# Strassen's product for an attention block's output projection, a third PSUM bank pair for the scores, and a bias added later

## The chip, the cores and the metric

The kernel runs on one core of one Trainium2 chip. Time is the device's microseconds from the first to the last instruction of one execution; the comparisons use several executions of each kernel. A core has TensorE (PE; matrix products, whose weight loads are listed apart as PEld), VectorE (DVE), ScalarE (ACT), GpSimd (POOL), and SyncE (SP), which here issues all transfers between memory and the on-chip buffer SBUF. TensorE writes to PSUM, which has eight banks of 128 x 512 float32; the kernel uses them as four pairs.

## The reference, cut to what matters

Two layers follow one another, on a batch of 8 images of 512 channels and 32 x 32 = 1024 tokens, all in float32:

```python
def layer(x, gn_w, gn_b, qkv_w, qkv_b, proj_w, proj_b):      # x: 8 x 512 x 1024
    xn = groupnorm(x) * gn_w + gn_b                          # 8 groups in layer 0, 32 in layer 1
    q, k, v = split(qkv_w @ xn + qkv_b)                      # each 512 x 1024, 8 heads of 64
    p = softmax(q_h^T k_h / 8)                               # per head, 1024 x 1024
    o_h = v_h p^T                                            # 64 x 1024 per head
    return proj_w @ o + proj_b + x                           # 512 x 512 times 512 x 1024
```

One image in one layer is a *unit*; there are 16. The matmuls of one unit are three projections of 512 x 512 by 512 x 1024, the attention of eight heads, and the output projection of the same size.

## The kernel before

Each unit runs in three stages: q, k and v; then the output projection of the unit before it; then this unit's attention. The output projection is late by one stage so that its last inputs, which need a transfer, have time to arrive.

q, k and v are computed by one level of Strassen's product (Winograd's form): the weights and the input are cut into 2 x 2 blocks and combined, seven block products are made instead of eight, and the outputs are sums of them. `blocks` does this for all three; `left` and `right` hold the seven operands on each side.

```python
    def blocks(name, left, right, tokens, c11, others, done):
        bx, by, bz = apair[0], sbank[0], sbank[1]
        def products(bank, k, start, stop):
            a, b = left[k], right[k]
            for i in range(4 if tokens else 2):
                # ... dst: a half of the bank pair
                for c in range(2):
                    at, moving = (b, a) if tokens else (a, b)
                    nc.tensor.matmul(dst, at[:, c, ts(i, P)], moving[:, c, :], ...)     # L284
            done()
        products(bx, 1, True, False)
        p1 = work(accpool, "acc", "p1")
        nc.scalar.copy(p1, bx)
        products(by, 6, True, False)
        u2 = work(trpool, "tr", "u2")
        nc.vector.tensor_add(u2, by, p1)
        products(bx, 2, False, True)
        c11(bx)
        products(by, 7, False, False)
        u3 = work(ppool, "p", "u3")
        nc.vector.tensor_add(u3, by, p1)
        products(bz, 5, True, False)
        others(1, 1, bz, u3)
        products(by, 4, False, True)
        others(1, 0, by, p1)
        products(bz, 3, False, True)
        others(0, 1, bz, u2)
```

The output projection is a plain product: four row blocks by two halves of the tokens, each the sum of four matmuls, and each evacuated with bias and residual in one VectorE instruction.

```python
    def project(w, after):
        for o in range(CC):                       # CC = 4
            for h in range(NH):                   # NH = 2
                bank = turns[2 + g % 2 + 4 * (g // 2 % 2)]
                for c in range(CC):
                    nc.tensor.matmul(bank, w.wproj[:, c, ts(o, P)], w.ao[c][:, ts(h, FD)],   # L381
                                     start=(c == 0), stop=(c == CC - 1))
                cols = w.res[o][:, ts(h, FD)]
                w.evac = nc.vector.scalar_tensor_tensor(                                      # L389
                    cols, bank, vec[:, l, PB, o : o + 1], cols, ALU.add, ALU.add)
                after(g)                          # the next unit's group statistics, one at a time
                g += 1
            nc.sync.dma_start(dst[o * P : (o + 1) * P, :], w.res[o])                          # L394
```

The residual's four tiles come from `ppool`, four buffers of 128 x 1024, which also hold the exponentials of attention and the `u3` of q, k and v. The last unit has no stage after it; `project_last` (L403) makes all sums but the last of four terms first, while the last inputs are prepared.

Attention has 64 steps: eight chunks (a pair of heads, half of the queries) of eight key blocks (`t`). A step makes scores for its keys, their exponential on ScalarE, and, one step later, the product with v. Scores alternate between two bank pairs; products of a chunk accumulate in one of the other two.

```python
        def scores(s):
            bank = sbank[s % 2]
            before = [state["exp"][s - 2]] if s >= 2 else []
            if s == 0:
                before += w.last["q"] + w.last["k"]
            gate(*before)
            # four matmuls of 64 x 64 x 512                                                   # L440
            p = ppool.tile([P, 2, FD], F32, tag="p", name=f"p_{u}_{s}")
            state["exp"][s] = nc.scalar.activation(p, bank, AF.Exp, scale=SCALE)              # L448
            return p
        # products(s, p): four matmuls of 64 x 64 x 512 into apair[c % 2]                     # L467
        # summed(s, p): sums of the exponentials on VectorE                                   # L484, L486
        # evacuate(c): ScalarE copy (L492) and VectorE addition (L493) into w.ao
        prev = None
        for s in range(n_chunks * NT):
            c, t = divmod(s, NT)
            p = scores(s)
            if prev is not None:
                products(s - 1, prev)
            if t == 0 and c > 0:
                evacuate(c - 1)
                transposed(c - 1)                                                             # L499
            if t == 2 and c > 0:
                reduced(c - 1)                    # L509; after a pair of chunks: transfers L515
            if c % NH == 1 and t == 0 and c > 1:
                reciprocals(c // NH - 1)          # small VectorE work, transfers L537, L542
            if c % NH == 1 and t == 6 and c > 1:
                divide(c // NH - 1)                                                           # L549
            if c % NH == 1 and t == 7 and 1 < c < n_chunks - 1:
                add_bias(c // NH - 1, 0)          # ScalarE, V's bias                         # L556
            if c % NH == 0 and t == 1 and c > 2:
                add_bias(c // NH - 2, 1)
            summed(s, p)
            at_step(s, state)                     # the next unit's group norm, a piece a step
            prev = p
        products(n_chunks * NT - 1, prev)
        evacuate(n_chunks - 1)
```

`at_step` makes the next unit's means (chunk 0, step 3) and variances (chunk 0, step 6) by small matmuls (L193), its scales in chunk 1, and applies them in chunks 2 to 5.

The end of the program, after the last unit's attention:

```python
    old.res = load_res(old.u)                     # four transfers, L109
    old.wproj = wproj
    project_last(old, rest)
```

Of the kernel before, what the change touches and what calls it, by code (L numbers as in the profile page):

```python
# [18 lines left out]
P = 128  # L19
# [13 lines left out]
def fast_path(ctx, tc, x, qkv_wT, proj_wT, vecs, groups, out, flag):  # L33
# [12 lines left out]

    nc = tc.nc
# [8 lines left out]
    BL = 32  # L56
# [9 lines left out]
    aopool = pool("aopool", CC)  # L66
# [7 lines left out]
    rbpool = pool("rbpool", 2)  # L74
# [56 lines left out]
    def mix_weights(l, mats, engine):  # L131
# [4 lines left out]
        for i, a in enumerate(mats):  # L136
# [13 lines left out]
    def mix_x(u, xn):  # L150

        b11, b12 = xn[:, :2, :FD], xn[:, :2, FD:]
        b21, b22 = xn[:, 2:, :FD], xn[:, 2:, FD:]
        t1, t2, t4 = (
            tpool.tile([P, 2, FD], F32, tag=f"t{k}", name=f"t{k}_{u}") for k in (1, 2, 4)
        )
        sub = nc.vector.tensor_sub
        parts = (
            lambda: sub(t1, b12, b11), lambda: sub(t2, b22, t1),
            lambda: sub(t4, b21, t2), lambda: sub(b12, b22, b12),  # L160
        )
        return {1: b11, 2: b21, 3: b22, 4: t4, 5: t1, 6: t2, 7: b12}, parts

    def load_proj(l):
        w = wpool.tile([P, CC, C], F32, tag="wproj", name=f"wproj_{l}")
        nc.sync.dma_start(w, proj_wT[l].rearrange("(c p) o -> p c o", p=P))
        return w
# [100 lines left out]
    def blocks(name, left, right, tokens, c11, others, done):  # L268
# [3 lines left out]
        bx, by, bz = apair[0], sbank[0], sbank[1]  # L272

        def products(bank, k, start, stop):
# [14 lines left out]
            done()  # L289

        def work(pool, tag, k):
            return pool.tile([P, 2, FD], F32, tag=tag, name=f"{k}_{name}")
# [3 lines left out]
        nc.scalar.copy(p1, bx)  # L296
        products(by, 6, True, False)
        u2 = work(trpool, "tr", "u2")
        nc.vector.tensor_add(u2, by, p1)
        products(bx, 2, False, True)  # L300
        c11(bx)
        products(by, 7, False, False)
        u3 = work(ppool, "p", "u3")
        nc.vector.tensor_add(u3, by, p1)
        products(bz, 5, True, False)
        others(1, 1, bz, u3)
        products(by, 4, False, True)
        others(1, 0, by, p1)
        products(bz, 3, False, True)
        others(0, 1, bz, u2)  # L310

    def projections(w, rest):
# [7 lines left out]
        def done():  # L320
            nonlocal g
            g += 1
            for part in rest.get(g, ()):
                part()

        for sel, bias in (("q", QB), ("k", KB)):
# [24 lines left out]
            blocks(f"{sel}_{u}", left, w.right, False, c11, others, done)  # L351
# [17 lines left out]
        blocks(f"v_{u}", w.lefts[2], w.right, True, v11, v_others, done)  # L369

    def project(w, after):
# [5 lines left out]
        for o in range(CC):  # L377
            for h in range(NH):
                bank = turns[2 + g % 2 + 4 * (g // 2 % 2)]
                for c in range(CC):  # L380
                    nc.tensor.matmul(  # L381
                        bank,
                        w.wproj[:, c, ts(o, P)],
                        w.ao[c][:, ts(h, FD)],
                        start=(c == 0),
                        stop=(c == CC - 1),
                    )
                cols = w.res[o][:, ts(h, FD)]
                w.evac = nc.vector.scalar_tensor_tensor(  # L389
                    cols, bank, vec[:, l, PB, o : o + 1], cols, ALU.add, ALU.add  # L390
                )
                after(g)
                g += 1
            nc.sync.dma_start(dst[o * P : (o + 1) * P, :], w.res[o])  # L394

    def project_last(w, rest):
# [4 lines left out]
        def products(g, c):  # L401
            o, h = divmod(g, NH)
            nc.tensor.matmul(  # L403
                turns[g], w.wproj[:, c, ts(o, P)], w.ao[c][:, ts(h, FD)],
# [17 lines left out]
    def attention(w, at_step):  # L422
# [3 lines left out]
        w.ao = [aopool.tile([P, N], F32, tag="ao", name=f"ao_{u}_{pr}") for pr in range(CC)]  # L426
        n_chunks = CC * NH
        state = {"exp": {}, "free": [[], []], "acc": {}}

        def scores(s):  # L430
            c, t = divmod(s, NT)
            pr, qh = divmod(c, NH)
            bank = sbank[s % 2]
            before = [state["exp"][s - 2]] if s >= 2 else []
            if s == 0:
                before += w.last["q"] + w.last["k"]
# [11 lines left out]
            state["exp"][s] = nc.scalar.activation(p, bank, AF.Exp, scale=SCALE)  # L448
            return p

        def products(s, p):
# [4 lines left out]
            if s == 0 and w.evac_before is not None:  # L456
                before.append(w.evac_before)
            if t == 0:
                before += state["free"][c % 2]
            if s == 0:  # L460
                before += w.last["v"]
# [26 lines left out]
        def evacuate(c):  # L488
# [4 lines left out]
            i1 = nc.vector.tensor_add(w.ao[pr][:, ts(qh, FD)], banks[1], tmp)  # L493
# [26 lines left out]
        def reciprocals(pr):  # L520
            def work(name):
                return small.tile([BL, 2 * BL], F32, tag=name, name=f"{name}_{u}_{pr}")
# [24 lines left out]
        def divide(pr):  # L547
            col = u * CC + pr
            nc.vector.scalar_tensor_tensor(  # L549
                w.ao[pr], w.ao[pr], 1.0, state["rb"], ALU.mult, ALU.mult,  # L550
# [3 lines left out]
        def add_bias(pr, h):  # L554
            cols = w.ao[pr][:, ts(h, FD)]
# [4 lines left out]
        prev = None  # L560
        for s in range(n_chunks * NT):
            c, t = divmod(s, NT)
            p = scores(s)
            if prev is not None:
                products(s - 1, prev)
# [9 lines left out]
            if c % NH == 1 and t == 7 and 1 < c < n_chunks - 1:  # L575
                add_bias(c // NH - 1, 0)
            if c % NH == 0 and t == 1 and c > 2:
                add_bias(c // NH - 2, 1)
            summed(s, p)
            at_step(s, state)  # L580
            prev = p
        products(n_chunks * NT - 1, prev)
# [12 lines left out]
        return lambda: reciprocals(CC - 1), divide_last  # L595
# [5 lines left out]
    mats = load_weights(0)  # L601
    wproj = load_proj(0)
# [356 lines left out]
```

## Time and profile before

| | |
|---|---|
| time of three executions | 3423.61, 3425.54, 3425.72 us (median 3425.54) |
| span of the profiled execution | 3422.5 us, TensorE's granted clock 0.999 |
| matmuls L467, products with v | 8192 records, 1118.3 us busy |
| matmuls L440, scores | 8192 records, 1116.1 us busy |
| matmuls L381, output projection | 960 records, 414.4 us busy |
| exponentials L448 | 1024, mean 1024 ns |
| additions L486 | 768, mean 1223 ns |
| biased evacuations L389 (128 x 512) | 120, mean 750 ns |
| additions L493 (128 x 512) | 128, mean 688 ns |
| V's bias L556 | 128, mean 720 ns |
| store of 256 KB, issue to landing | 2.0 us median |
| store of 512 KB, issue to landing | 2.6 us median |

A float32 matmul appears as two records. The spacing of starts, not the length of a record, is what a matmul costs in a stream, because matmuls overlap. Idle time in a row of the profile names what ended it; time that the chain of waits gives to TensorE can only be shortened by giving TensorE less to do.

### The profile page before, as it was taken

How to read it: one execution, taken by the hardware profiler on the slowest of the kernel's cores; microseconds unless marked ns; L12 is line 12 of the kernel's file. 1: busy time of each engine (PE TensorE's matmuls, PEld its weight loads, DVE VectorE, ACT ScalarE, POOL GpSimd, SP SyncE). 2: the span in 40 equal slices, each digit the busy share in tenths (PEclk: the TensorE clock that was granted, in tenths of full speed). 3: DMA queues.
4: the chain of work that ended last, by engine and by line, in shares of the span. 5: the costliest groups of instructions: out<-in, count | busy, mean ns of one | idle time of the engine just before them, and what ended most of it. 6: DMA issues, size and time to landing. Idle time of an engine off the chain costs nothing.

```text
span 3422.5 us, 50906 instructions
## 1 busy us (share of the span) xinstructions
PE 3381.2 (99%) x21122; PEld 1679.7 (49%) x21122; DVE 2211.3 (65%) x2790; ACT 1374.0 (40%) x1533; POOL 32.6 (1%) x32
## 2 busy tenths in 40 slices
PE   8999999999999999999999999999999999999999
PEld 4445454454544545455454554545445454454543
DVE  4865938658385583856838568384673946749466
ACT  1632606336062360723517235172451714417144
POOL 0000000000000000001000000000000000000000
PEclk9999999999999999999999999999999999999999
DMA  2111020111101111012120111101111011110102
GB/s 76 36 35 56 21 74 20 32 56 27 68 20 32 56 33 68 15 32 93 39 74 15 32 63 33 62 15 38 56 33 62 15 38 56 33 62 15 38 32 70
DMA packets 57674, 148.21 MB, mean 43 GB/s; under 512 B 19808, under 2 KB 20064, under 8 KB 57440
## 3 DMA queue, kind: packets, MB, share of 16 engines
q1 hardware_dynamic: 57440, 144.90, 12.6%
q8 instruction: 171, 2.80, 0.3%
q14 instruction: 63, 0.52, 0.0%
HBM read 109.21 MB, written 34.08 MB: 42 GB/s over the span
## 4 chain that ended last, share of the span: by engine, by line
PE 96%; DVE 1%; ACT 1%; issue 1%; DMA 1%; SPq 0%; POOL 0%; DVEq 0%
PE a L467 25%; PE s L440 25%; PE s L284 24%; PE a L381 12%; PE a L284 10%; ACT p L448 1%; DVE acc L486 0%; DMA xn<-x_dram 0%; DMA drec<-rec 0%; DVE tr L499 0%; DVE stats L181 0%; DMA rb<-drec 0%; PE s L403 0%; PE a L403 0%; PE a L193 0%
## 5 line engine op out<-in xcount | busy, mean ns | idle before, releaser
L448 ACT ACTIVATE p<-s 128x1024 f32<-128x1024 f32 x1024 | 1046.9, 1024 | 1159.2 <-PE s L440 1149.5
L467 PE MATMUL a<-p,v 64*64 64x512 f32 x8192 | 1118.3, 590 | 15.8 <-ACT p L448 13.7
L440 PE MATMUL s<-q,k 64*64 64x512 f32 x8192 | 1116.1, 590 | 0.3 <-DVE v L364 0.3
L486 DVE TENSOR_TENSOR acc<-acc,p 128x1024 f32<-128x1024 f32 x768 | 938.9, 1223 | 118.0 <-ACT p L448 77.4
L467 PEld LDWEIGHTS a<-p,v 64*64 64x64 f32 x8192 | 385.3, 131 | 524.2 <-ACT p L448 406.8
L440 PEld LDWEIGHTS s<-q,k 64*64 64x64 f32 x8192 | 413.6, 133 | 450.2 <-issue 449.1
L381 PE MATMUL a<-ao,wproj 128*128 128x512 f32 x960 | 414.4, 592 | 0.0
L381 PEld LDWEIGHTS a<-ao,wproj 128*128 128x128 f32 x960 | 182.4, 190 | 223.2 <-issue 222.4
L389 DVE SCALAR_TENSOR_TENSOR x<-a,vec,x 128x512 f32<-128x512 f32 x120 | 90.1, 750 | 272.8 <-PE a L381 272.8
L284 PE MATMUL a<-xn,w 128*128 128x512 f32 x512 | 234.0, 600 | 4.0 <-DVE xn L241 4.0
L284 PEld LDWEIGHTS a<-xn,w 128*128 128x128 f32 x512 | 96.8, 191 | 132.4 <-issue 113.0
L484 DVE TENSOR_TENSOR acc<-p,p 128x1024 f32<-128x1024 f32 x128 | 153.2, 1197 | 11.3 <-ACT p L448 11.3
L499 DVE STREAM_TRANSPOSE tr<-acc 128x1024 f32<-128x1024 f32 x128 | 158.0, 1235 | 0.0
L509 DVE TENSOR_REDUCE red<-tr 128x32 f32<-128x1024 f32 x128 | 154.4, 1207 | 0.6
L556 ACT ACTIVATE ao<-ao,vec 128x512 f32<-128x512 f32 x128 | 89.1, 720 | 110.3 <-DVE ao L549 110.3
L493 DVE TENSOR_TENSOR ao<-a,tmp 128x512 f32<-128x512 f32 x128 | 88.1, 688 | 60.1 <-ACT tmp L492 60.1
L296 ACT COPY p_k<-a 128x1024 f32<-128x1024 f32 x16 | 16.2, 1012 | 254.4 <-PE a L284 254.4
L296 ACT COPY p_v<-a 128x1024 f32<-128x1024 f32 x16 | 16.2, 1012 | 251.8 <-PE a L284 235.8
L284 PE MATMUL a<-w,xn 128*128 128x256 f32 x512 | 115.7, 379 | 0.0
L284 PE MATMUL s<-xn,w 128*128 128x512 f32 x256 | 115.1, 592 | 0.0
L284 PE MATMUL s<-t,s2w 128*128 128x512 f32 x256 | 115.1, 592 | 0.0
L284 PE MATMUL s<-t,w 128*128 128x512 f32 x256 | 115.1, 592 | 0.0
(100 smaller groups left out, 2167.6 us busy)
## 6 DMA issues: line engine op xcount, KB each, us to landing
rb<-drec SPq DMA_DIRECT2D x128, 256.0 KB, 3.9
xn<-x_dram SPq DMA_DIRECT2D x32, 512.0 KB, 4.8
x<-x_dram SPq DMA_DIRECT2D x32, 512.0 KB, 3.2
mid<-x SPq DMA_DIRECT2D x32, 512.0 KB, 2.6
xn<-mid SPq DMA_DIRECT2D x32, 512.0 KB, 4.9
x<-mid SPq DMA_DIRECT2D x32, 512.0 KB, 3.5
out_dram<-x SPq DMA_DIRECT2D x28, 512.0 KB, 2.6
w<-qkv_wT_dram SPq DMA_DIRECT2D x6, 1024.0 KB, 11.4
```

Of the source, the lines that this page charges most:

```text
L284: nc.tensor.matmul(dst, at[:, c, ts(i, P)], moving[:, c, :], start=start and c == 0 and not (tokens and i % 2), stop=stop and c == 1, skip ...
L381: nc.tensor.matmul(bank, w.wproj[:, c, ts(o, P)], w.ao[c][:, ts(h, FD)], start=(c == 0), stop=(c == CC - 1),)
L389: w.evac = nc.vector.scalar_tensor_tensor(cols, bank, vec[:, l, PB, o : o + 1], cols, ALU.add, ALU.add)
L440: nc.tensor.matmul(bank[e * H : (e + 1) * H, j, :], w.k[pr][j * H : (j + 1) * H, t * P + e * H : t * P + (e + 1) * H], w.q[pr][j * H : (j ...
L448: state["exp"][s] = nc.scalar.activation(p, bank, AF.Exp, scale=SCALE)
L467: nc.tensor.matmul(banks[r][j * H : (j + 1) * H, :], w.v[rows, t, lo : lo + D], p[rows, j, :], start=(t == 0), stop=(t == NT - 1),)
L484: nc.vector.tensor_add(acc, state["first"], p)
L486: nc.vector.tensor_add(acc, acc, p)
L493: i1 = nc.vector.tensor_add(w.ao[pr][:, ts(qh, FD)], banks[1], tmp)
L499: nc.vector.transpose(tr, state["acc"].pop(c))
L509: nc.vector.tensor_reduce(red[:, :, qh, :], state["tr"].rearrange("p j (f i) -> p j f i", i=BL), AX.X, ALU.add)
L556: nc.scalar.activation(cols, cols, AF.Identity, bias=vec[:, units[u][0], VB, pr : pr + 1])
```

## The change

The output projection (all units but the last) goes through `blocks` as well: seven block products in place of eight. The right operand's combinations (`mix_right`) are made on VectorE while k is computed, the weights' ones once per layer, and the bias and the residual are added to the partial sums in SBUF. Results are stored in halves. The combinations overwrite one block of the weights, so the last unit, which keeps the plain product, loads its weights again.

```diff
-        bx, by, bz = apair[0], sbank[0], sbank[1]
+        bx, by, bz = apair[0], sbank[0], apair[1]
...
     def project(w, after):
...
-        for o in range(CC):
-            for h in range(NH):
... (the plain product and its evacuation, shown above)
+        def plus(to, o, cols, more):
+            return nc.vector.scalar_tensor_tensor(
+                to, cols, vec[:, l, PB, o : o + 1], more, ALU.add, ALU.add
+            )
+        def done(sums):
+            nonlocal g
+            g += 1
+            for i in range(2):
+                if g == 2:
+                    u2 = sums[1][:, i, :]
+                    plus(u2, i, w.res[i][:, FD:], u2)
+                elif g == 4:
+                    u3 = sums[2][:, i, :]
+                    plus(u3, 2 + i, w.res[2 + i][:, FD:], u3)
+                elif g == 5:
+                    p1 = sums[0][:, i, :]
+                    plus(p1, 2 + i, w.res[2 + i][:, :FD], p1)
+            after(g)
+        def store(o, h):
+            nc.sync.dma_start(dst[o * P : (o + 1) * P, ts(h, FD)], w.res[o][:, ts(h, FD)])
+        def c11(bank):
+            for i in range(2):
+                cols = w.res[i][:, :FD]
+                plus(cols, i, bank[:, i, :], cols)
+                store(i, 0)
+        def others(r, h, bank, more):
+            for i in range(2):
+                o = 2 * r + i
+                w.evac[h] = nc.vector.tensor_add(
+                    w.res[o][:, ts(h, FD)], bank[:, i, :], more[:, i, :]
+                )
+                store(o, h)
+        w.evac = [None, None]
+        blocks(f"o_{w.u}", w.left, w.right_o, False, c11, others, done, (rbpool, "rb"))
```

Attention's first six scores rotate through three bank pairs, and the products follow two steps behind in the first chunk; the last score goes to a free pair ahead of two products. This lets exponentials run ahead where the pipeline fills and empties. V's bias moves from the steps around a chunk's start to steps 2 and 3, and the group statistics' small matmuls move from chunk 0 to chunk 1, because their bank pair is the one borrowed.

```diff
-            bank = sbank[s % 2]
-            before = [state["exp"][s - 2]] if s >= 2 else []
+            if s < 6:
+                bank = (*sbank, apair[1])[s % 3]
+                before = state["exp"][s - 3 : s - 2] if s >= 3 else []
+            elif s == n_steps - 1:
+                bank = apair[0]
+                before = state["free"][0]
+            else:
+                bank = sbank[s % 2]
+                before = [state["exp"][s - (3 if s < 8 else 2)]]
             if s == 0:
-                before += w.last["q"] + w.last["k"]
+                before = before + w.last["q"] + w.last["k"] + (w.evac_before[:1] or w.last["v"])
+            elif s == 2:
+                before = before + w.evac_before
...
+        follow = {s: [s - 1] for s in range(NT, n_steps)}
+        follow.update({s: [s - 2] for s in range(2, NT - 1)})
+        follow[NT - 1] = [NT - 3, NT - 2]
+        follow[n_steps - 2] = []
+        follow[n_steps - 1] = [n_steps - 3, n_steps - 2]
...
-            if c % NH == 1 and t == 7 and 1 < c < n_chunks - 1:
-                add_bias(c // NH - 1, 0)
-            if c % NH == 0 and t == 1 and c > 2:
-                add_bias(c // NH - 2, 1)
+            if c % NH == 0 and t in (2, 3) and c > 2:
+                add_bias(c // NH - 2, t - 2)
...
-        return lambda: reciprocals(CC - 1), divide_last
+        w.right_o, mixing = mix_right(f"o_{u}", *w.ao)
+        return {4: [lambda: reciprocals(CC - 1)], 10: [divide_last], 12: mixing[:2], 14: mixing[2:]}
...
-            project(old, lambda g: stats_of(g - 2))
+            stats_after = {3: (0, 1, 2), 4: (3,), 6: (4, 5), 7: (6, 7)}
+            project(old, lambda g: stats_of(*stats_after.get(g, ())))
...
-            if c == 0 and t == 1:
+            if c == 1 and t == 1:
                 aggregate()
-            elif c == 0 and t == 3:
-                means(abank[2 * pair], *(free or [w.evac_before]))
+            elif c == 1 and t == 3:
+                means(abank[2 * pair], *free)
-            elif c == 0 and t == 6:
+            elif c == 1 and t == 5:
                 variances(abank[2 * pair], *free)
...
     old.res = load_res(old.u)
-    old.wproj = wproj
-    project_last(old, rest)
+    old.wproj = load_proj(1, "w0")
+    project_last(old, [part for g in (4, 10) for part in rest[g]])
```

The keys 4, 10, 12 and 14 count block products of q, k and v (seven each): the last pair's reciprocals, its division, and the two halves of the mixing are placed there. The attention outputs `w.ao` become two tiles of 128 x 2 x 1024, and the working tile `u3` of the projection takes the buffer of the broadcast reciprocals (`rbpool`), which goes from two buffers to one.

## The prediction

> **What bounds the kernel now.** I read the page's busy times and its chain of waits first, then busy time by stage, then the order of time at the seams between stages.
>
> ```profile
> PE 3381.2 (99%) x21122; PEld 1679.7 (49%) x21122; DVE 2211.3 (65%) x2790; ACT 1374.0 (40%) x1533; POOL 32.6 (1%) x32
> ...
> PE a L467 25%; PE s L440 25%; PE s L284 24%; PE a L381 12%; PE a L284 10%; ACT p L448 1%; DVE acc L486 0%; DMA xn<-x_dram 0%; DMA drec<-rec 0%; DVE tr L499 0%; DVE stats L181 0%; DMA rb<-drec 0%; PE s L403 0%; PE a L403 0%; PE a L193 0%
> ```
>
> TensorE is the bound: 99% busy, and 96% of the chain. The chain's shares name what can be shortened: attention (L440, L467) half, the q, k and v products (L284) a third, the output projection (L381) an eighth. The third unit by stages (window, length, then busy time of PE, PEld, DVE, ACT, POOL):
>
> ```profile
> 416.99:489.43 72.44, 72.44 (x226) 42.76 (x226) 27.99 (x36) 9.61 (x13) 0.00 (x0) 1.00 0.11 37
> 489.43:516.90 27.47, 27.47 (x69) 11.88 (x70) 9.47 (x13) 0.00 (x0) 0.00 (x0) 1.00 0.35 134
> 516.90:629.06 112.16, 111.18 (x1033) 50.97 (x1033) 100.03 (x125) 76.31 (x83) 1.01 (x1) 1.00 0.07 21
> ```
>
> A unit takes 72.44 + 27.47 + 112.16 = 212.07 us. The first two stages are gapless. In attention a group of eight matmul records starts every 0.858 us, so 64 steps of two groups need 109.85; 2.3 us are lost. The TensorE timeline of this stage says where (start, length):
>
> ```profile
> 516.83 1.95 PE L440 MATMUL s<-q,k 64*64 64x512 f32 x16
> 519.26 1.09 PE L467 MATMUL a<-p,v 64*64 64x512 f32 x8 [0.49 <-ACT p L448]
> ...
> 573.53 1.13 PE L440 MATMUL s<-q,k 64*64 64x512 f32 x8
> 574.72 1.09 PE L467 MATMUL a<-p,v 64*64 64x512 f32 x8
> ...
> 626.54 1.07 PE L467 MATMUL a<-p,v 64*64 64x512 f32 x8
> 627.98 1.09 PE L467 MATMUL a<-p,v 64*64 64x512 f32 x8 [0.37 <-ACT p L448]
> ```
>
> Start to start, less 0.858 per group: the first product comes 0.71 late (2.43 for two groups), one in the middle 0.33 late (another at 602.49 by 0.28), the last 0.58 late. Other units show the same within 0.01, with two exceptions (0.10 and 0.74 in the middle). The middle one is ScalarE's doing:
>
> ```profile
> 571.26 1.02 ACT L448 ACTIVATE p<-s 128x1024 f32<-128x1024 f32 x1 [0.69 <-PE s L440]
> 572.83 0.72 ACT L556 ACTIVATE ao<-ao,vec 128x512 f32<-128x512 f32 x1 [0.54 <-DVE ao L549]
> 573.46 1.00 ACT L448 ACTIVATE p<-s 128x1024 f32<-128x1024 f32 x1
> 574.36 0.57 ACT L492 COPY tmp<-a 128x512 f32<-128x512 f32 x1
> 574.83 1.04 ACT L448 ACTIVATE p<-s 128x1024 f32<-128x1024 f32 x1
> ```
>
> V's bias (L556) waits for the division, runs just before a chunk's first exponential (L448), and the evacuation copy (L492) follows at once: the next exponential is late, and the products that read it.
>
> The end of the kernel, in order of time, before the change:
>
> ```profile
> 3386.30 5.42 PE L403 MATMUL s<-ao,wproj 128*128 128x512 f32 x12
> 3391.15 1.80 SPq L515 DMA_DIRECT2D lt<-red  x3
> ...
> 3393.06 1.94 SPq L109 DMA_DIRECT2D x<-mid  x4
> ...
> 3407.41 1.98 PE L403 MATMUL s<-ao,wproj 128*128 128x512 f32 x4 [0.24 <-ACT ao L556]
> ```
>
> The last projection starts at once at 3386.30, because its weights are there; 24 matmuls fill the time until the last divided pair arrives at 3407.41. SyncE issues in program order: the residual's four loads follow the sums' transfers. TensorE's first products after its idle beginning, and the same form later:
>
> ```profile
> 16.96 5.84 PE L284 MATMUL a<-xn,w 128*128 128x512 f32 x8 [3.96 <-DVE xn L241]
> ...
> 26.08 3.60 PE L284 MATMUL a<-xn,w 128*128 128x512 f32 x8
> ```
>
> **What the skill says.** "TensorE: Matmul & The Clock Gate", Part 1: after an idle window of about 3.4 us the array falls to half clock, until about 3.4 us of work. The trace agrees: 5.84 us where 3.43 is the later spacing, 2.4 more. "VectorE: DVE Perf Modes", the section on the errata: an fp32 tensor_tensor of N elements takes (N+151)/0.96 ns, so 1224 for 1024; L486 has 1223. "DMA: Bandwidth & Descriptors", Bandwidth: a 1 MB load takes 6.15 us; the lone weight load at 1790 landed in 6.5.
>
> **The change part by part.**
>
> *Projection.* Now 8 groups of 4 matmuls, 64 records at 0.429, 27.47 us. Strassen's level has 7 products of 4 matmuls (2 row blocks by 2 contraction blocks, 128x512): 8 records each. The same form in q and k starts every 3.43 us, so 7 x 3.433 = 24.03. Saved 3.44, in 15 units (the last keeps its own projection): **51.5 us**.
>
> What it adds stays beside TensorE. VectorE per projection: two sums of 1024 (2 x 1.22), two outputs from the first block (2 x 0.75), six bias-and-residual additions in SBUF (6 x about 0.72), six closing additions (6 x 0.69), eight statistics (8 x 0.68): about 18 us in 24. By product: the sum after the second is due before the fourth overwrites, 3.4 us later, and takes 1.2; the busiest group (the third, 1.4 + 3 x 0.65) fills its 3.43. The four mixing subtractions (4 x 1.22) fall in k's products, where VectorE is under half busy. ScalarE adds one copy of 1.01. No stall from these.
>
> *Attention's start.* Three scores come before the first product. The third starts 1.72 after the first and ends at 2.58; the first exponential ends at 2.17 (1.15 after its score's start, 1.02 long), and the matmul needs 0.25 more: 2.42. The 0.71 vanishes in 15 units: **10.6 us**. The third score needs the last bank evacuated: two additions from 0.10 to about 1.4, in time for 1.72. The first unit has no projection; its first score now waits for V's last evacuation (1.23 from 0.1 after the product), about 1.55 late where 0.70 was lost: **minus 0.9**.
>
> *Attention's end.* The last score moves ahead of two products. Its exponential follows the previous one, ends 2.2 after the score's start, and the last product is due at 2.58: 0.58 becomes almost nothing, in 15 units **8.6 us**.
>
> *V's bias* at steps 2 and 3 of a chunk: ScalarE then has 1.02 + 0.63 per 1.72, and the copy is past. The two delays go, 16 x 0.61 with the two exceptions: **10 us**.
>
> *Group statistics* move one chunk later. In the first unit TensorE waited 0.95 for them at 113.08; there the matmul now has a chunk more: **1 us**. In the others the second small matmul comes a step earlier (5, not 6) in a chunk with evacuation, transpose and reduce. VectorE: addition at 2.7 us into the chunk, transpose 3.3, sum 4.5, aggregate 5.5, reduce 5.9, two sums to 9.4, four small operations to about 10.2; the matmul is due at 10.3. Just in time; I allow **minus 1** for all units.
>
> *The tail.* Mixing overwrites a block of the weights in place, so the last unit reloads them, and that load stands in the program after attention and after the residual's four loads. SyncE cannot reach it before 3393.06 + 1.94 = 3395.0 on the old axis. The last of the four loads (2 MB) landed at 3400.8 there; 1 MB behind at the rate of the first loads (4 MB of weights in 11 us, an estimate from their issue and landing) adds 2.8: 3403.7. The 24 matmuls, which started at 3386.30, start at about 3403.9, cold: 24 x 0.858 = 20.6, plus 2.4 for the half clock, ends at 3426.9; the eight that remained began at 3407.41. The tail grows by **19.5 us**.
>
> Sum: 51.5 + 10.6 - 0.9 + 8.6 + 10 + 1 - 1 - 19.5 = 60.3, rounded to 60 for small losses: 3425.5 - 60 = **3366 us**, 1.7% less.
>
> **Rivals.**
>
> *The stores take the place of the first wait.* The residual's tiles share four buffers with the exponentials, and the first two tiles are now stored last: after the last product (0.1), one addition (0.7) and a 256 KB store (2.0 by the page) the buffer is free at 2.9 us, not at 1.15. If the first exponential gets that buffer, TensorE idles 1.7 at each start: 15 x 1.7 = 26 us back, 3392. Against it: the waits of the transfer queue show the second, third and fourth residual load waiting for q's, k's and v's working tile in turn, so the buffer free longest is given out; that is now tile 2's, stored one product earlier and landed 0.6 before. The third exponential then gets the late one, natural start 3.2 against 2.9.
>
> *The reload is hidden.* Only if it were issued before attention ends: 3346. The program order of SyncE speaks against it.
>
> *VectorE becomes the bound.* It is 65% busy and gains about 17 us a unit in a shorter unit, some 75%. If it fell behind at the seams, 0.5 us a unit: 3374.
>
> **Range and chances.** The projection's term is sure within 1 us, seams within 6, the tail within 4; the rivals stretch mostly upward. 8 in 10: 3355 to 3381. Two per cent is 3357, beyond my sum by 9 us: faster by over 2% 0.13, within 2% 0.85, slower by over 2% 0.02.
>
> **What would show it.** L284 instead of L381 in a stage of 24.0 us. First product 2.58 after the first score; no wait at the last. Unit period near 212.07 - 3.44 - 0.71 - 0.58 - 0.61 = 206.7. Between the last attention product and the first L403-like matmul a gap near 17 us that ends with the weights' transfer. Wrong would be: exponentials waiting on a store at each start, small matmuls (L193) waiting on VectorE, or no gap in the tail.

## The result, and the profile after

| | before | after |
|---|---|---|
| median of four executions | 3424.66 us | 3363.11 us |
| lowest to highest | 3423.61 to 3425.72 | 3362.13 to 3364.76 |
| span of the profiled execution | 3422.5 us | 3360.4 us |

The ratio of after to before is 0.982, with an interval from 0.980 to 0.984: 1.8% less time. The prediction was 3366.

The page of the changed kernel: busy time of each engine, then the chain of waits.

```profile
PE 3316.9 (99%) x21002; PEld 1645.9 (49%) x21002; DVE 2376.2 (71%) x2978; ACT 1394.1 (41%) x1548; POOL 49.2 (1%) x32
...
PE a L288 26%; PE a L514 26%; PE s L486 25%; PE s L288 19%; PE a L486 1%; PE s L437 0%; PE a L437 0%; DVE acc L533 0%; DMA wproj_w<-proj_wT_dram 0%; DMA xn<-x_dram 0%; DVE tr L546 0%; SPq L110 0%; PE a L196 0%; DVE red L556 0%; DVE acc L531 0%
```

TensorE is still the bound. The plain projection's 12% has left the chain and its products now stand under L288, the line that also makes q, k and v: 45% in place of 34%. VectorE rose to 71%, yet the whole chain holds about 1% of it. One transfer is new: the weights' (`wproj_w`). In the list of TensorE's waits (us in total, times, longest) the kernel before has this row for the products with v, and the changed kernel has none:

```profile
PE a L467 <- ACT p L448: 13.7, 32, 0.5
```

The third unit again by stages (window, length, busy time of PE, PEld, DVE, ACT, POOL, then clock, DMA share, GB/s):

```profile
410.41:482.76 72.35, 72.35 (x227) 42.67 (x226) 33.50 (x42) 9.62 (x13) 0.00 (x0) 1.00 0.11 37
482.76:506.88 24.12, 24.12 (x57) 10.45 (x55) 15.40 (x21) 1.01 (x1) 0.00 (x0) 1.00 0.41 153
506.88:617.14 110.26, 110.26 (x1033) 49.95 (x1032) 99.01 (x123) 76.65 (x83) 1.98 (x1) 1.00 0.08 21
```

The unit takes 206.73 us in place of 212.07. The first two stages together lost 3.44 (99.91 to 96.47), attention 1.90 (112.16 to 110.26), which is 0.71 + 0.58 + 0.61.

Attention's first and last moments in that unit, from the timeline:

```profile
506.88 1.95 PE L486 MATMUL s<-q,k 64*64 64x512 f32 x16
506.99 1.29 DVE L422 TENSOR_TENSOR x<-a,u_o 128x512 f32<-128x512 f32 x2 [0.95 <-PE a L288]
508.04 1.94 ACT L494 ACTIVATE p<-s 128x1024 f32<-128x1024 f32 x2 [20.59 <-PE s L486]
508.65 1.04 PE L486 MATMUL a<-q,k 64*64 64x512 f32 x8
509.51 1.04 PE L514 MATMUL a<-p,v 64*64 64x512 f32 x8
...
614.40 2.81 PE L514 MATMUL a<-p,v 64*64 64x512 f32 x24
617.14 1.12 PE L288 MATMUL a<-xn,w 128*128 128x512 f32 x2
```

The third score now goes to the pair `a`. It starts 1.77 after the first, within 0.05 of a gapless stream; the two additions that empty its bank end at 508.28, in time. The first product comes 2.63 after the first score and waits for nothing. At the other end the last three products are one row of 24 records, with no wait before the last. The Trainium skill ("VectorE: DVE Perf Modes", the section on the errata) puts a float32 tensor_tensor at (N+151)/0.96 ns, 691 for 512 elements, under a heading on operations that read SBUF. These additions read one operand from PSUM, and two in a row took 1.29, so 645 each, a little less than the page's figure.

ScalarE in the middle of the same attention:

```profile
562.35 1.02 ACT L494 ACTIVATE p<-s 128x1024 f32<-128x1024 f32 x1 [0.69 <-PE s L486]
563.27 0.58 ACT L539 COPY tmp<-a 128x512 f32<-128x512 f32 x1
564.06 1.02 ACT L494 ACTIVATE p<-s 128x1024 f32<-128x1024 f32 x1 [0.22 <-PE s L486]
565.78 1.02 ACT L494 ACTIVATE p<-s 128x1024 f32<-128x1024 f32 x1 [0.69 <-PE s L486]
566.70 0.71 ACT L603 ACTIVATE ao<-ao,vec 128x512 f32<-128x512 f32 x1
```

The copy (L539) and the bias (L603) no longer stand around one exponential. Each takes part of a pause of its own, and the exponentials keep their spacing of 1.72.

The tail, TensorE and SyncE in order of time, and then the landings of two transfers (issues, KB, us from issue to landing):

```profile
3302.03 2.75 PE L514 MATMUL a<-p,v 64*64 64x512 f32 x24
...
3312.08 1.94 SPq L110 DMA_DIRECT2D x<-mid  x4
3314.12 0.69 SPq L169 DMA_DIRECT2D wproj_w<-proj_wT_dram  x1
3314.90 0.47 SPq L584 DMA_DIRECT2D drec<-rec  x1
...
3322.79 7.82 PE L437 MATMUL s<-ao,wproj_w 128*128 128x512 f32 x12 [18.00 <-DMA wproj_w<-proj_wT_dram]
...
3330.45 5.31 PE L437 MATMUL a<-ao,wproj_w 128*128 128x512 f32 x12
```

```profile
drec<-rec SPq DMA_DIRECT2D x1, 8.0 KB, 8.0
...
wproj_w<-proj_wT_dram SPq DMA_DIRECT2D x1, 1024.0 KB, 8.6
```

SyncE issues the weights only after the sums' transfers and the residual's four, 9.4 us after attention has ended; they land 8.6 later. TensorE idles 18.00, and its next twelve records take 7.82 where the twelve after them take 5.31: 2.51 more at the lower clock (granted clock 0.50 in the first 3.2 us). From the place of the last projection's start to the end of the span it is 3360.4 - 3304.7 = 55.7 us; before it was 3422.5 - 3386.3 = 36.2. The tail grew by 19.5.

### The profile page after: what moved, and what is told of

It is laid out like the page before. It is cut to its first block, busy times and chain, and to the rows that moved or that the text cites. A ratio compares the mean times of both kernels' runs of the same rounds, so it can differ in the third digit from the quotient of the medians.

```text
span 3360.4 us, 51078 instructions
## 1 busy us (share of the span) xinstructions
PE 3316.9 (99%) x21002; PEld 1645.9 (49%) x21002; DVE 2376.2 (71%) x2978; ACT 1394.1 (41%) x1548; POOL 49.2 (1%) x32
## 3 DMA queue, kind: packets, MB, share of 16 engines
HBM read 110.26 MB, written 34.08 MB: 43 GB/s over the span
## 4 chain that ended last, share of the span: by engine, by line
PE 98%; DVE 1%; DMA 0%; issue 0%; SPq 0%; ACT 0%; POOL 0%; DVEq 0%
PE a L288 26%; PE a L514 26%; PE s L486 25%; PE s L288 19%; PE a L486 1%; PE s L437 0%; PE a L437 0%; DVE acc L533 0%; DMA wproj_w<-proj_wT_dram 0%; DMA xn<-x_dram 0%; DVE tr L546 0%; SPq L110 0%; PE a L196 0%; DVE red L556 0%; DVE acc L531 0%
## 5 line engine op out<-in xcount | busy, mean ns | idle before, releaser
L494 ACT ACTIVATE p<-s 128x1024 f32<-128x1024 f32 x976 | 998.3, 1024 | 815.8 <-PE s L486 781.8
L514 PE MATMUL a<-p,v 64*64 64x512 f32 x8192 | 1101.3, 589 | 0.1
L486 PE MATMUL s<-q,k 64*64 64x512 f32 x7808 | 1059.4, 590 | 1.4 <-DVE v L375 1.4
L486 PEld LDWEIGHTS s<-q,k 64*64 64x64 f32 x7808 | 385.8, 133 | 437.1 <-issue 434.6
L288 PE MATMUL a<-xn,w 128*128 128x512 f32 x512 | 233.4, 599 | 4.0 <-DVE xn L244 4.0
L288 PEld LDWEIGHTS a<-xn,w 128*128 128x128 f32 x512 | 96.6, 191 | 131.9 <-issue 127.4
L300 ACT COPY p_o<-a 128x1024 f32<-128x1024 f32 x15 | 15.2, 1012 | 244.2 <-PE a L288 244.2
L288 PE MATMUL a<-w,xn 128*128 128x256 f32 x512 | 115.7, 379 | 0.0
L288 PE MATMUL s<-xn,w 128*128 128x512 f32 x256 | 115.2, 592 | 0.4 <-DVE u_q L304 0.4
L288 PE MATMUL s<-x_t,s2w 128*128 128x512 f32 x256 | 115.1, 592 | 0.0
L288 PE MATMUL a<-x_t,s1w 128*128 128x512 f32 x256 | 115.1, 592 | 0.0
L288 PE MATMUL s<-x_t,w 128*128 128x512 f32 x256 | 115.1, 592 | 0.0
L288 PE MATMUL a<-xn,s4w 128*128 128x512 f32 x256 | 115.1, 592 | 0.0
L288 PE MATMUL a<-ao,wproj_wproj 128*128 128x512 f32 x240 | 107.9, 592 | 0.0
```

The source lines that it names most:

```text
L288: nc.tensor.matmul(dst, at[:, c, ts(i, P)], moving[:, c, :], start=start and c == 0 and not (tokens and i % 2), stop=stop and c == 1, skip ...
L486: nc.tensor.matmul(bank[e * H : (e + 1) * H, j, :], w.k[pr][j * H : (j + 1) * H, t * P + e * H : t * P + (e + 1) * H], w.q[pr][j * H : (j ...
L494: exp = nc.scalar.activation(p, bank, AF.Exp, scale=SCALE)
L514: nc.tensor.matmul(banks[r][j * H : (j + 1) * H, :], w.v[rows, t, lo : lo + D], p[rows, j, :], start=(t == 0), stop=(t == NT - 1),)
```

## The experiments

All edits are against the changed kernel. In three groups on three chips the kernel before ran beside them at 3423.29, 3424.20 and 3424.10; each ratio is to the one on the same chip, while the differences in us are to the changed kernel's 3363.11. The theory was the prediction's sum of terms. Its rivals were stores that take the place of the first wait, a hidden reload, and VectorE as the bound.

**The reload, asked for before attention.** The buffer `w0` has been free since the last unit's q, k and v.

```diff
             old.res = load_res(old.u)
+        if u == 2 * B - 1:
+            w.wproj = load_proj(1, "w0")
...
-    old.wproj = load_proj(1, "w0")
```

> The last unit's weights are loaded again before its attention and not after it; nothing else changes. My theory (the reload stands alone in the tail: 18 us of waiting and about 2.5 us of half clock) expects 3343 us, 20 less than the changed kernel, and no gap before the last projection. Rival: the tail is set by the last pair's sums, their transfers and the division, and the reload hides behind them; then the gap only moves to a later wait and the time stays above 3355.

Measured: 3344.56 (3343.14 to 3345.53), ratio 0.977, interval 0.975 to 0.979; 18.5 less than the changed kernel. The timeline of its tail:

```profile
3306.22 5.42 PE L437 MATMUL s<-ao,wproj_w 128*128 128x512 f32 x12
...
3321.77 5.31 PE L437 MATMUL a<-ao,wproj_w 128*128 128x512 f32 x12
3328.01 1.98 PE L437 MATMUL s<-ao,wproj_w 128*128 128x512 f32 x4 [0.93 <-ACT ao L603]
```

The gap is gone, so the reload's place in the program, and not the transfer itself, cost the tail. From the last projection's start to the end of the span it is 3342.7 - 3306.2 = 36.5 us, so in the traces 19.2 of the 19.5 come back. After 24 gapless matmuls the wait for the last divided pair (L603) shows again: 0.93 here, 0.24 in the kernel before. In the changed kernel the longer wait for the weights had covered it.

**V's bias back in its old steps.**

```diff
-            if c % NH == 0 and t in (2, 3) and c > 2:
-                add_bias(c // NH - 2, t - 2)
+            if c % NH == 1 and t == 7 and 1 < c < n_chunks - 1:
+                add_bias(c // NH - 1, 0)
+            if c % NH == 0 and t == 1 and c > 2:
+                add_bias(c // NH - 2, 1)
```

> V's bias goes back to the last step of a chunk and step 1 of the next; the rest stays changed. My theory (ScalarE runs bias, exponential and copy in a row just before a product needs its exponential) expects two late products of about 0.3 us in each of 16 units, 10 us in all: 3373. Rival: the later group norm (steps 4 and 6) or the third bank pair already gave ScalarE the room, and the bias's place costs nothing: 3363.

The later group norm that this names is part of the change: it is applied at steps 4 and 6 of a chunk instead of 2 and 5.

Measured: 3374.70 (3373.33 to 3375.54), ratio 0.986, interval 0.984 to 0.987: 11.6 more. ScalarE's timeline:

```profile
563.74 0.72 ACT L603 ACTIVATE ao<-ao,vec 128x512 f32<-128x512 f32 x1 [0.54 <-DVE ao L596]
564.37 1.00 ACT L494 ACTIVATE p<-s 128x1024 f32<-128x1024 f32 x1
565.27 0.58 ACT L539 COPY tmp<-a 128x512 f32<-128x512 f32 x1
565.74 1.04 ACT L494 ACTIVATE p<-s 128x1024 f32<-128x1024 f32 x1
```

Bias, exponential, copy and exponential stand shoulder to shoulder again. In the same trace the product after the score of 564.44 starts at 565.63, 0.33 late, and one at 593.40 is 0.28 late: the two delays of before. Over the whole trace 32 products are late at these two places, two in each of 16 units, by 11.0 us together.

**Two bank pairs for the scores, products one step behind, as before the change.**

```diff
-            if s < 6: ...
-            elif s == n_steps - 1: ...
-            else: ...
+            bank = sbank[s % 2]
+            before = [state["exp"][s - 2]] if s >= 2 else []
...
-        follow = {s: [s - 1] for s in range(NT, n_steps)}   # and four more lines
+        follow = {s: [s - 1] for s in range(1, n_steps)}
```

> Scores keep to two bank pairs all through, with products one step behind; the rest stays changed. My theory expects the first product 0.7 us late again in 16 units and the last 0.58 late in 15 whose end is on the path: 3363 + 10.6 + 8.5 = 3382. Rival: most of the gain came from elsewhere and the third pair is worth under 5 us: below 3368.

Measured: 3380.24 (3379.31 to 3381.95), ratio 0.987, interval 0.986 to 0.989: 17.1 more. The timeline of the third unit's attention start:

```profile
508.54 1.95 PE L477 MATMUL s<-q,k 64*64 64x512 f32 x16
...
510.87 1.09 PE L505 MATMUL a<-p,v 64*64 64x512 f32 x8 [0.38 <-ACT p L485]
```

The first product is 2.33 after the first score where two groups need 1.72, so 0.61 late; the last is 0.62 late (617.49 to 618.97 for one group). Fifteen times 1.23 is 18.5, near the 17.1 of the times. TensorE's list of waits has the 32 of before again:

```profile
PE a L505 <- ACT p L485: 11.6, 32, 0.4
```

**The plain projection, with all else of the change.** The weights then stay whole, so there is no reload either; the seams, the bias and the statistics' small matmuls stay as changed, while the eight statistics on VectorE go back to their places behind the plain products.

```diff
-        blocks(f"o_{w.u}", w.left, w.right_o, False, c11, others, done, (rbpool, "rb"))
+        for o in range(CC):
+            for h in range(NH):
+                ... # four matmuls, then scalar_tensor_tensor with bias and residual
+                after(g); g += 1
+            nc.sync.dma_start(dst[o * P : (o + 1) * P, :], w.res[o])
```

> The output projection is the plain product again (32 matmuls, no mixing, and so no reload of the weights at the end); third bank pair and bias stay changed. My theory expects 15 x 3.44 = 51.6 us more for the matmuls and 20 less without the reload: 3363 + 51.6 - 20 = 3395, each projection 27.5 us long. Rival: VectorE's added work made the changed kernel's stages longer than their matmuls, and taking it away returns part of it: below 3388.

Measured: 3395.88 (3394.86 to 3396.62), ratio 0.992, interval 0.990 to 0.994. Both it and the first experiment have a tail without a reload, so their difference is the product with the VectorE work that goes with it: 3395.88 - 3344.56 = 51.3, or 3.42 for each of 15 units. The stage is 27.4 long in its trace.

**Does VectorE have room?** The two additions that form the partial sums `u2` and `u3` of the projection are made twice: 2.44 us more in each of 15 projections, after the second and the fourth of seven block products.

```diff
-        nc.vector.tensor_add(u2, by, p1)
+        for _ in range(2 if name[0] == "o" else 1):
+            nc.vector.tensor_add(u2, by, p1)
...                                                # the same for u3
```

> The two sums of 128 x 1024 after the second and fourth block product of the output projection are made twice each: 2.44 us more VectorE work in 15 projections, in the middle of them. My theory (VectorE has room there, and only a wait of TensorE counts) expects the changed kernel's time within 2 us: 3363 to 3365. Rival: VectorE is so nearly full in this stage that added work shows in the time: up to 15 x 2.44 = 37 us, 3400.

Measured: 3364.27 (3362.97 to 3366.04), ratio 0.982, interval 0.981 to 0.984. Some 37 us of added work leave a difference of 1.2, within the executions' spread. In the third unit the stage's last additions still start 0.11 after the first score, as in the changed kernel, with 0.72 of idle time before them in place of 0.95:

```profile
508.45 1.29 DVE L424 TENSOR_TENSOR x<-a,u_o 128x512 f32<-128x512 f32 x2 [0.72 <-PE a L288]
```

So VectorE has room for this much here; how much more it would bear, no run shows.

**The same engine at the seam.** The projection's last two additions, those that empty the bank of the third score, are made twice.

```diff
-                w.evac[h] = nc.vector.tensor_add(...)
+                for _ in range(2 if (r, h) == (0, 1) else 1):
+                    w.evac[h] = nc.vector.tensor_add(...)
```

> Only the two closing additions after the last block product are made twice: 1.35 us more VectorE work in 15 projections, at the seam to attention. My theory: the third score waits for these additions, which end at 1.4 and are due at about 1.6 after the projection; they end at 2.8 now, so the third score comes about 1.2 late: 15 x 1.2 = 18 us, 3381. Rival: the seam has more room than that (the first exponentials are still running), and the time stays within 5 us: below 3368.

Measured: 3382.28 (3381.91 to 3384.07), ratio 0.988, interval 0.987 to 0.990: 19.2 more. Timeline at the start of the third unit's attention:

```profile
508.92 1.95 PE L487 MATMUL s<-q,k 64*64 64x512 f32 x16
509.03 2.74 DVE L423 TENSOR_TENSOR x<-a,u_o 128x512 f32<-128x512 f32 x4 [0.95 <-PE a L288]
...
511.92 1.09 PE L487 MATMUL a<-q,k 64*64 64x512 f32 x8 [1.05 <-DVE x L423]
```

```profile
PE a L487 <- DVE x L423: 16.6, 15, 1.9
```

The row of additions grew by 1.45. The third score starts 3.00 after the first instead of 1.72, so 1.28 late; 15 times that is 19.2, and the second view, TensorE's waits, has this wait 15 times. The difference of 0.17 is all the slack the seam had. Added work of 1.45 us costs nearly its full length here, and 2.44 us up to the stage's middle cost nothing that shows. VectorE's total share does not tell these apart; the place does.

**A late buffer for the first exponential, first attempt.** Two small GpSimd fills take buffers of `ppool` ahead of the exponentials, so that the first exponential would be handed a tile stored last.

```diff
+        for i in range(2 if w.evac_before else 0):
+            skip = ppool.tile([P, 2, FD], F32, tag="p", ...)
+            nc.gpsimd.memset(skip[:, 0, :4], 0.0)
```

> Two unused tiles are taken from the exponentials' pool and given back just before attention (a 4-element fill each on GpSimd, which is idle), so that the first exponential gets the buffer of the residual tile that is stored last; the rest is the changed kernel. My theory (a first exponential waits for that store, landing about 2.9 us after the projection, where it could start at 1.15) expects 1.7 us more in 15 units: 3363 + 26 = 3389, with the exponential released by the store. Rival: the buffer's turn doesn't matter, because the stores land before the exponentials need them: 3363.

Measured: 3364.82 (3361.52 to 3366.66), ratio 0.982, interval 0.981 to 0.984: no change. The timelines of the third unit and of the unit at the change of layers say why:

```profile
506.69 0.26 POOL L610 MEMSET skip<- 128x4 f32 x2 [178.65 <-DMA mid<-x]
```

```profile
1545.30 1.94 ACT L494 ACTIVATE p<-s 128x1024 f32<-128x1024 f32 x2 [24.02 <-POOL skip L610]
1546.46 1.99 PE L514 MATMUL a<-p,v 64*64 64x512 f32 x8 [2.75 <-ACT p L494]
```

In the third unit both fills run together as soon as one store has landed, ahead of the last additions at 507.16. At the change of layers GpSimd was not idle, as I had assumed: it was combining the next layer's weights until 1545.00, and there the first exponential waits for a fill. So the exponential took a buffer that a fill had used. The likely reading is that fills and exponential went through the same early buffer one after the other and the late buffers were left for later; which buffer each got stands in no view. In no unit does a store release the first exponential, so the condition I wanted never arose, and the attempt decides nothing on the rival. The one late fill cost time of its own: the product at 1546.46 starts 5.75 after its first score, where 2.63 is usual, and after these 2.75 us of idleness two groups took 3.40 in place of 1.72.

**The same question, by the stores.** The first halves of tiles 2 and 3 are stored after those of tiles 0 and 1, so that every buffer comes free late.

```diff
-                store(o, h)
+                if (r, h) != (1, 0):
+                    store(o, h)
+            if (r, h) == (0, 1):
+                store(2, 0)
+                store(3, 0)
```

> In each output projection the stores of the first halves of residual tiles 2 and 3 are held back until those of tiles 0 and 1 are issued; the rest is the changed kernel. Now no residual tile is given back early, and the first exponential has to take tile 0's buffer, whose store lands about 2.9 us after the projection. My theory expects the first product 1.6 to 1.7 us late in 15 units, the exponential released by the store: 3363 + 25 = 3388. Rival: the stores land before the exponentials need the buffers whatever their order: 3363.

Measured: 3386.84 (3386.20 to 3387.56), ratio 0.989, interval 0.988 to 0.991: 23.7 more. Its timeline, and TensorE's waits:

```profile
507.88 1.95 PE L490 MATMUL s<-q,k 64*64 64x512 f32 x16
...
510.89 1.94 ACT L498 ACTIVATE p<-s 128x1024 f32<-128x1024 f32 x2 [22.45 <-DMA mid<-x]
...
512.06 1.09 PE L518 MATMUL a<-p,v 64*64 64x512 f32 x8 [1.38 <-ACT p L498]
```

```profile
PE a L518 <- ACT p L498: 20.9, 15, 1.7
```

In the third unit the first exponential is released by a store, and TensorE waits for an exponential in 15 places, one for each projection. The first product comes 4.18 after the first score where 2.58 is gapless; 15 times 1.60 is 24.0. The rival's mechanism is real and its size was right. The changed kernel escapes it because it stores tiles 2 and 3 one product earlier: in the trace with the fills a store had landed by 506.69, 0.36 before the first score and about 1.5 before the exponential needs its buffer.

**The early reload, and the first unit's first score gated only by its own bank.** V's evacuation that empties the first score's bank is the third of four; the third score takes the wait for all of them.

```diff
-                before = ... + (w.evac_before[:1] or w.last["v"])
+                before = ... + (w.evac_before[:1] or w.last["v"][2:3])
             elif s == 2:
-                before = before + w.evac_before
+                before = before + (w.evac_before or w.last["v"])
... # and the early reload of the first experiment
```

> The early reload of the weights, and in the first unit the first score waits only for the evacuation of its own bank (the third of V's four), the third score for all of them. Theory: 20 us from the reload and about 1.4 from the first unit's first score: 3341 to 3342. Rival for the second part: the first unit's products wait for V's last evacuation anyway, and only the reload's 20 us come: 3343.

Measured: 3341.96 (3341.62 to 3343.51), ratio 0.976, interval 0.975 to 0.978. The first unit's start in the changed kernel, and then here:

```profile
87.43 3.62 PE L288 MATMUL a<-s4w,xn 128*128 128x256 f32 x16
92.41 1.95 PE L486 MATMUL s<-q,k 64*64 64x512 f32 x16 [1.36 <-DVE v L375]
```

```profile
86.42 3.62 PE L288 MATMUL a<-s4w,xn 128*128 128x256 f32 x16
89.96 1.95 PE L486 MATMUL s<-q,k 64*64 64x512 f32 x16
...
92.59 1.04 PE L514 MATMUL a<-p,v 64*64 64x512 f32 x8
```

The first score follows V's last products after 3.54 instead of 4.98, and the first product comes 2.63 after it without a wait, so the rival for this part is out. The time alone would not settle it: the executions reach 3343. Against the early reload alone the median is 2.6 lower, of which the first unit gives 1.44; in these two traces the tail gives 0.8 of it back (37.3 us against 36.5), and most of the rest lies at the kernel's beginning, which the edit does not touch: the second row of q's products starts at 21.06 against 23.18.

**And the residual's loads after the reciprocals.** In the tail the small transfers that bring the last pair's reciprocals stood behind the residual's 2 MB.

```diff
-    old.res = load_res(old.u)
-    project_last(old, [part for g in (4, 10) for part in rest[g]])
+    def load_last():
+        old.res = load_res(old.u)
+    project_last(old, rest[4] + [load_last] + rest[10])
```

> The version with the early reload and the shorter wait in the first unit, with the last unit's four residual loads issued after the reciprocals' two transfers and not before them. In that version the last projection still waited 1.65 us for the last divided pair, whose small transfer stood behind 2 MB of residual. Theory: the reciprocals' transfer lands in about 1.4 us in place of 5.3, the pair is ready before the 24 matmuls end, and the 1.65 us go: 3340. Rival: the residual arrives too late for the first closing addition and the gain is given back: 3342 or more.

Measured: 3341.11 (3340.93 to 3342.29), ratio 0.976, interval 0.975 to 0.977. Against the version before it the executions overlap, and the times alone do not settle 0.9 us. The two timelines do show what moved in the tail, first without and then with this edit:

```profile
3312.36 0.32 SPq L584 DMA_DIRECT2D drec<-rec  x1
3318.21 1.12 SPq L589 DMA_DIRECT2D rb<-drec  x2
...
3325.07 1.99 PE L437 MATMUL s<-ao,wproj_w 128*128 128x512 f32 x4 [1.65 <-ACT ao L603]
```

```profile
3313.87 0.31 SPq L584 DMA_DIRECT2D drec<-rec  x1
3315.31 1.12 SPq L589 DMA_DIRECT2D rb<-drec  x2
...
3324.75 1.88 PE L437 MATMUL s<-ao,wproj_w 128*128 128x512 f32 x4
```

The broadcast (`rb`) must wait until the reciprocals (`drec`) have landed: 5.85 us without the edit, 1.44 with it. TensorE's wait of 1.65 for the last pair is gone. From the start of the last projection to the end of the span it is 37.3 us without and 35.5 with the edit. The span shrank by only 0.3, since this execution reached its tail 1.5 later. That comes from the kernel's beginning: the first row of q's products started 0.62 later (16.42 against 15.80), and it took 6.45 us to the next row where the other execution took 5.26. Counted from that next row (22.87 and 21.06) to the end of the span, the edit saves 2.1.

## Why the prediction was right

The mechanisms held, and the sum of 60.3 met a measured 61.6 (3424.66 - 3363.11). By its terms (a minus is time saved):

| term | predicted | measured | where |
|---|---|---|---|
| projection | -51.5 | -51.6, -51.3 | 15 x 3.44 from the stages; plain product against the early reload |
| attention's start and end | -19.2 | -17.1 | two bank pairs put back |
| V's bias | -10 | -11.6 | bias put back |
| first unit's first score | +0.9 | +0.8 | 0.61 lost there before, 1.44 after (4.98 - 3.54), each against a gapless start |
| statistics | -1 and +1 | -1 | the first unit's wait of 0.95 is gone; no new one in the trace |
| tail | +19.5 | +19.5 | from the last projection's place to the end |

Each "put back" is the difference of two medians whose executions spread by 2 to 3 us, on chips where the kernel before differs by up to 1.4, so the 2 us of the second row are not to be read further. In the third row the trace with the bias put back gives 11.0 by itself: its late products take 0.6 to 0.8 a unit, as the prediction had it, except 1.45 in the first unit. In the traces the three gains of attention show at their predicted sizes together (1.90 a unit).

*Projection.* Right in size. The work on VectorE was placed right too: about 18 us were expected, and the stage has 15.40, with the last two additions (1.29) and two statistics (1.28) after its end, together 18.0.

*VectorE's share* was the mis-sized term, in the rival that made it the bound. I wrote that it gains about 17 us a unit; it gained (2376.2 - 2211.3) / 15 = 11.0. The 17 counts the eight statistics (5.4 us) as new, though the stage before had them as well. The rival would have fallen faster with the right number, and the time does not rest on it.

*The stores.* The argument that the buffer free longest is handed out, and that this is tile 2's, decided between 3366 and 3392. The changed kernel's first exponential starts 1.16 after its score, as it should with a free buffer, and holding the stores back gave the rival's 24 us. So the choice was right, and the reason given agrees with the changed kernel and with both experiments on its buffers, though no view names the buffer that was handed out. It was narrow: the early store has landed about 1.5 us before its buffer is needed.

*The tail.* The gap was put at 17.6 and measured 18.00; the half clock at 2.4 and measured 2.51. The Trainium skill ("TensorE: Matmul & The Clock Gate", Part 1) has this drop after an idle window of about 3.4 us; the tail's 18 us agree, but in the trace with the fills 2.75 us were enough (granted clock 0.51 in the 3.40 us that followed). The rival of a hidden reload (3346) is what the early load makes true (3344.56), so program order alone separated the two.

*Luck in the tail.* The 2.4 was in part luck. It sets the length of a row, 5.84, against a spacing, 3.43; from start to start (16.96 to 22.64) the row took 5.68, so 2.25 more, and this price varies (last section). The 19.5 to the digit is luck too: the last eight matmuls began 20.1 later in the tail than before, and what follows them was 0.6 shorter. Nothing rests on the 6.15 us for 1 MB that the prediction sets beside the 6.5 of a load: the page gives it for loads issued from GpSimd, as the span in which the DMA engines are busy, while SyncE issues here and the 6.5 runs from issue to landing.

*Not foreseen:* in the second unit a product of q waits 0.38 for VectorE's partial sum, which comes after work left over from the first unit's attention. Before the change the same sum ended at 215.09 and was needed at 215.20, so there was no room for an attention that ends sooner. It costs half a microsecond, once.

## What to carry to other kernels

A change that saves work in every repetition can give back a quarter of it in the one place where it spoils what had been kept ready: about 81 us were gained here in the units and 19.5 lost in the tail, and one moved load brought back 18.5. Price an engine's extra work by where its end is waited for: 2.44 us of VectorE up to the middle of a stage were free, and 1.45 at its end cost 1.28. An experiment must show in its own trace that the condition it was meant to make came about, or its equal time proves nothing.

## What was not expected of the hardware

A transfer's size says little of its latency when others stand before it on the same queue: the reciprocals' 8 KB took 1.4 us in the median. In the tail they took 8.0 behind 3 MB of residual and weights, and with only the residual's 2 MB ahead 5.9 passed until the transfer that needs them was issued. The Trainium skill ("DMA: Bandwidth & Descriptors", "Two DMAs through the same engine are not ordered") says that descriptors within one queue of one DMA engine start in order; all these transfers are issued on SyncE's queue, so the order fits.

The price of the lower clock is not a fixed sum, and it was no larger after 18 us of idleness in the tail than at the kernel's beginning. There TensorE has done only eight short records and is idle for 3.95 us before its first row of q's products. In the twelve traces of this case that row takes 4.95 to 6.52 us to the start of the next one, where 3.43 is the later spacing: 1.5 to 3.1 more. In the seven traces with the gap in the tail, 17.3 to 18.3 us of idleness, the first twelve records take 6.86 to 8.21 where the next twelve take 5.15: 1.7 to 3.1 more. The profile shows a granted clock of 0.50 in the changed kernel's tail, but 1.00 at its beginning, so there the lower clock is inferred from the spacing alone. Either place can move one execution against another by more than a microsecond.
